# The first attention's maxima step in another ring of banks, and its transposed scores in front of the scores

## The chip, the cores and the metric

The kernel runs on one core of one Trainium2 chip. The time is device microseconds of that core. A run is one execution of the whole program; the times given are of three runs, and one further execution was taken with the hardware profiler.

## The reference

The program is a small stack of layers over x of shape 2 x 512 x 512 in float32: four attentions, each followed by a feed-forward layer, every layer on a layer norm of x and added to x. The change touches only the first attention, which has 32 heads of 4 latent columns and no mask:

```python
C_q = x @ Wq_d + bq_d                                   # 12 columns
C_kv = x @ Wkv_d + bkv_d                                # 4 columns
q = (C_q @ W_qk + b_qk).reshape(b, s, 32, 4)
scores = jnp.einsum('bqhd,bkd->bhqk', q, C_kv) / 2
attn = jax.nn.softmax(scores, axis=-1)
V = (C_kv @ Wv_u + bv_u).reshape(b, s, 32, 16)
out = jnp.einsum('bhqk,bkhd->bqhd', attn, V).reshape(b, s, 512)
return out @ Wo + bo
```

## The kernel before

Scores are computed twice. A score matmul has queries in its rows and keys in its columns (128 x 512); VectorE takes each row's negated maximum from it, and nothing else is kept. A transposed score has keys in its rows and queries in its columns; it goes through exp on ScalarE and is then the moving operand of the matmuls with the values. For the exp to see the maximum already taken off, the maxima themselves are transposed and added to the queries, as further rows of the moving operand qm.

The heads are handled four at a time, a *quartet*: 16 quartets, u = 0 to 15 (two batches, two halves, four each). The four heads g = 0 to 3 of a quartet lie on 32 partitions each, and a matmul of a score or of a transposed score reads only the 32 rows of its head.

- `score(u, qt, g)` (L586): a matmul of 32 rows (L589) into a bank of the S ring, then on VectorE a reduce of that bank into one column of `nm[u % 2]` (L597).
- `split(u)` (L601): two small GpSimd steps on the maxima (L606, L607), after the quartet's last score.
- `maxima(u)` (L611): four transposes of `nm` into one bank (L615), one more matmul that adds the queries (L199, in `correct`), and a copy on ScalarE to `qm[u]` (L618).
- `transposed(u, kc, g)` (L621): a matmul of 32 rows (L627) of `qm[u]` into a bank of the T ring, then exp on ScalarE (L630).
- `values(u, kc)` (L632): four matmuls of the values with the exps (L637), into a bank of their own.

The eight PSUM banks are dealt out by hand: the S ring has banks 0, 1, 2, the T ring 3, 4, 5, the values bank 6, and bank 7 takes other work. `own_bank` goes around a ring; a matmul into a bank waits until the reduce, exp or copy that read the bank's last content is done.

TensorE's instructions are issued in the order in which they are written here (`manual_schedule`); the other engines' order is the scheduler's. Twelve half rows of scores (`next_scores`, two matmuls each) are issued ahead; then every quartet has eight steps. A step has two scores of a later quartet, two transposed scores of this one, and then either a `values` of four heads or a slice of other work (`slices`: heads of the second batch, sums of weights, the feed-forward layer's first products, layer norms; two or three matmuls that fill up, if there is nothing). In even steps the scores are of heads 0 and 1 and the transposed scores of heads 2 and 3, in odd steps the other way around. Scores run 12 half rows ahead, so the maxima of quartet u + 1 are complete after step 3 of quartet u; `maxima(u + 1)` stands in step 6, and `transposed(u + 1, ...)` begins in step 0 of the next quartet. "Step 0" below is always that of the quartet that follows.

Of the kernel before, what the change touches and what calls it, by code (L numbers as in the profile page):

```python
# [38 lines left out]
B, S, D = 2, 512, 512  # L39
# [389 lines left out]
def attn_latent_small(k, a):  # L429
# [9 lines left out]
    with ExitStack() as ctx:  # L439
# [134 lines left out]
        last = len(quartets) - 1  # L574
# [7 lines left out]
        def own_bank(kind):  # L582
            turns[kind] = (turns[kind] + 1) % 3
            return k.held[:, banks[kind][turns[kind]]]

        def score(u, qt, g):  # L586
            b, half, i = quartets[u]
            ps = own_bank("S")
            nc.tensor.matmul(  # L589
                ps,  # L590
                qs[b][rows[g], 4 * half + i, bass.ts(qt, P)],
                keys[b][rows[g]],
                start=True,
                stop=True,
            )
            at = 32 * g + HIGH
            k.latest = nc.vector.tensor_reduce(  # L597
                nm[u % 2][:, qt, at : at + 1], ps, AX.X, ALU.max, negate=True
            ).ins

        def split(u):  # L601


            every = nm[u % 2].rearrange("p t (g e) -> p t g e", g=4)
            top = lp.tile([P, NT, 4], F32R, tag="top", name="top")
            nc.gpsimd.tensor_copy(top, every[:, :, :, HIGH])  # L606
            k.pooled = nc.gpsimd.tensor_tensor(  # L607
                every[:, :, :, LOW], every[:, :, :, HIGH], top.bitcast(F32), ALU.subtract
            ).ins

        def maxima(u):  # L611
            b, half, i = quartets[u]
            tp = own_bank("S")
            for qt in range(NT):
                nc.tensor.transpose(tp[:, bass.ts(qt, P)], nm[u % 2][:, qt], k.ident)  # L615
            k.correct(tp, unit, qs[b][:, 4 * half + i])
            t = lp.tile([P, S], F32R, tag="qm", name="qm")
            nc.scalar.copy(t, tp)  # L618
            qm[u] = t

        def transposed(u, kc, g):  # L621
            b, half, i = quartets[u]
            if (u, kc) not in probs:
                odd = kc % 2
                probs[u, kc] = lp.tile([P, 4, S], F32, tag="pT", name="pt") if odd else k.other()
            ps = own_bank("T")
            nc.tensor.matmul(  # L627
                ps, keys[b][rows[g], bass.ts(kc, P)], qm[u][rows[g]], start=True, stop=True
            )
            nc.scalar.activation(probs[u, kc][:, g], ps, AF.Exp)  # L630

        def values(u, kc):  # L632
            b, half, i = quartets[u]
            acc = k.held[:, of_values]
            pt = probs.pop((u, kc))
            for g in range(4):
                nc.tensor.matmul(  # L637
                    acc[rows[g]],
                    vals[b][:, kc, i],
                    pt[:, g],  # L640
                    start=(i == 0 and kc == 0),
                    stop=(i == 3 and kc == NT - 1),
                )
            if i == 3 and kc == NT - 1:
                raws[u] = one([P, S], "raw")
                nc.scalar.copy(raws[u], acc)
                extra.extend(following(u))
# [91 lines left out]
        def next_scores():  # L739
            at = next(scores, None)  # L740
            if at:
                u, qt, p = at
                for g in (2 * p, 2 * p + 1):
                    score(u, qt, g)
                if (qt, p) == (NT - 1, 1):
                    split(u)

        def run(pieces):
            for piece in pieces:
                for _ in piece:  # L750
                    pass

        def fill(n, bank):
            for _ in range(n):
                nc.tensor.matmul(k.held[:, bank], unit, keys[0], start=True, stop=True)

        def slices(cost):

            if not extra:
                fill(3, k.ring[-1])  # L760
            with tc.issue_after(first):
                while extra and cost > 0:
                    done = next(extra[0], None)
                    if done is None:
                        extra.pop(0)
                    else:
                        cost -= done
# [35 lines left out]
        with tc.manual_schedule(engines={mybir.EngineType.PE}):  # L803
            for n in range(12):
                next_scores()
                slices(1)
                fill(2, of_values)
                if n == 7:
                    with tc.issue_after(k.latest):
                        adapter_coefficients(k, a)  # L810
                if n == 8:
                    maxima(0)
            run(extra)
            extra = later
            k.ring = other
            for u in range(len(quartets)):
                if u == last:
                    k.ring = (0, 1, 2, 7)
                for step in range(8):
                    next_scores()  # L820
                    for g in (2, 3) if step % 2 == 0 else (0, 1):
                        transposed(u, step // 2, g)
                    if step == 6 and u < last:
                        maxima(u + 1)
                    if step % 2 == 0 and len(behind) > 1:
                        values(*behind.pop(0))
                        if u == last:
                            slices(1)
                    else:
                        slices(2 if u == last else 1)  # L830
                    if step % 2:
                        behind.append((u, step // 2))
            k.ring = (0, 1, 2, 3, 4, 5, 7)
            for at in behind:
                values(*at)
            run(extra)
# [4 lines left out]
def adapter_coefficients(k, a):  # L841

    nc = k.nc
    k.coef = k.const.tile([P, 1], F32, tag="coef", name="coef")
    starts = k.load_row(a["f0_starts"], 4, "f0_starts", dtype=I32)
    rows = k.load(a["c_lora"], [P, 4], "c_lora", 1)
    startf = k.sm(4, "startf", 1)
    nc.vector.tensor_copy(startf, starts)


    c = k.sm(4, "le", 1)
    nc.vector.tensor_scalar(c, startf, rows[:, 3:4], None, ALU.is_le)
    r = k.sm(3, "rank", 1)
    both = k.sm(2, "adapter", 1)
    nc.vector.tensor_tensor(both, c[:, 1:3], c[:, 2:4], ALU.mult)
    nc.vector.tensor_tensor(r[:, 0:2], c[:, 1:3], both, ALU.subtract)
    nc.vector.tensor_copy(r[:, 2:3], both[:, 1:2])
    nc.vector.tensor_tensor(r, r, rows[:, 0:3], ALU.mult)
    nc.vector.tensor_reduce(k.coef, r, AX.X, ALU.add)
# [1308 lines left out]
@with_exitstack  # L2168
def kernel(ctx: ExitStack, tc: tile.TileContext, a: dict, out: bass.AP):
    k = Block(ctx, tc, a["x"], out)  # L2170
    k.hold()
    block = attn_latent_small(k, a)
    bound = CausalBound(k, a)
    attn_gqa(k, a, bound, block)
    ffn_lora(k, a, block)
    attn_mla(k, a)
    k.release(ctx)
    with k.tc.tile_pool(name="f1", bufs=2) as own:
        experts = Experts(k, a, own)
        with k.tc.tile_pool(name="heads", bufs=1) as pool:  # L2180
            rooms = HeadRooms(k, a, pool)
            experts.first(rooms.fill)
            attn_mha(k, a, bound.register(), rooms, experts)
        experts.end()
# [168 lines left out]
```

## Time and profile before

| | us |
|---|---|
| median of 3 runs | 1969.8 |
| lowest and highest | 1969.27, 1971.89 |
| the profiled execution | 1968.03 |
| its span, first to last instruction | 1966.3 |
| TensorE busy in the span | 1926.5 |
| VectorE busy | 1372.1 |
| ScalarE busy | 933.6 |
| GpSimd busy | 1026.6 |
| mean granted TensorE clock | 0.999 |

In the profile PE is TensorE's matmuls, PEld its weight loads, DVE VectorE, ACT ScalarE, POOL GpSimd; L589 is line 589 of the kernel. A timeline row has the start in us, the time from start to end in us, engine, line, operation, what is written and read, shapes, and how many were merged; a bracket at the end tells how long the engine had been idle and what ended that. Matmuls overlap: the time from one matmul's start to the next one's, here called a slot, tells what it occupies TensorE for. A waits row has who waited, for whom, us in total, how often, and the longest. A windows row has, for each engine, its busy time and number of instructions in that stretch, then the granted clock and the DMA's share and rate.

The first attention's quartets run from about 42 to 255 us of the span.

### The profile page before, as it was taken

The numbers are of one execution on the slowest core, as the hardware profiler recorded it, in microseconds if no ns is written. First come the engines' busy times: TensorE is split into PE (matmuls) and PEld (weight loads), VectorE is DVE, ScalarE is ACT, GpSimd is POOL, SyncE is SP. The second block draws the span as 40 slices with busy tenths as digits, with TensorE's granted clock in tenths as the row PEclk, the third lists the DMA queues.
The fourth block names the chain that finished last, engine by engine and source line by source line (L and its number), as shares of the span: only waits on it lengthen the run. The fifth ranks groups of instructions, "written<-read, shape, count | busy, mean of one in ns | idle before, by whom it ended". The sixth has DMA issues, their size and how long they took to land.

```text
span 1966.3 us, 40477 instructions
## 1 busy us (share of the span) xinstructions
PE 1926.5 (98%) x15610; PEld 1194.0 (61%) x15610; DVE 1372.1 (70%) x3457; ACT 933.6 (47%) x2450; POOL 1026.6 (52%) x1122
## 2 busy tenths in 40 slices
PE   9989999999999999999999999999999999999999
PEld 5333356777777777777777545666565654654554
DVE  8889658767776676777765577777777756847853
ACT  3876624444444343444443166666666411541550
POOL 4332055776756667677763257565656556216221
PEclk9999999999999999999999999999999999999999
DMA  3010212222322322232223212020101002002001
GB/s 136 17 44 1 75 65 66 82 72 88 97 68 61 97 76 82 76 98 76 79 79 85 72 22 109 7 71 10 62 13 55 23 12 48 2 2 44 2 2 44
DMA packets 69296, 108.96 MB, mean 55 GB/s; under 512 B 13922, under 2 KB 48994, under 8 KB 62052
## 3 DMA queue, kind: packets, MB, share of 16 engines
q1 hardware_dynamic: 68804, 104.15, 18.0%
q8 instruction: 127, 2.08, 0.4%
q0 software_dynamic: 288, 2.10, 0.3%
q14 instruction: 77, 0.63, 0.1%
HBM read 80.00 MB, written 4.19 MB: 43 GB/s over the span
## 4 chain that ended last, share of the span: by engine, by line
PE 84%; DVE 6%; POOL 5%; issue 3%; ACT 2%; SPq 0%; DMA 0%; DVEq 0%; POOLq 0%; ACTq 0%
PE held L1004 13%; PE held L281 11%; PE held L1139 9%; PE held L190 9%; PE held L357 8%; PE held L637 3%; PE held L589 3%; PE held L1076 3%; PE held L473 2%; PE held L1498 2%; PE sc L190 2%; PE held L1495 1%; PE tp L1769 1%; DVE nm L597 1%; PE held L1496 1%
## 5 line engine op out<-in xcount | busy, mean ns | idle before, releaser
L302 ACT ACTIVATE room<-room,nmax 128x128 f32<-128x128 f32 (+3 forms) x384 | 212.7, 557 | 355.2 <-DVE nmax L292 352.7
L281 PE MATMUL held<-kT,q 128*32 128x32 f32 (+15 forms) x4096 | 262.6, 396 | 6.6 <-DVE invs L310 2.3
L292 DVE CUSTOM_DVE_ANT_0 room<-held,mask 128x128 f32<-128x128 f32 (+3 forms) x384 | 178.9, 488 | 63.1 <-PE held L281 57.7
L281 PEld LDWEIGHTS held<-kT,q 128*32 128x32 f32 x4096 | 143.1, 110 | 87.5 <-issue 34.7
L357 PE MATMUL held<-turned,vals 32*128 32x384 f32 (+7 forms) x2784 | 189.5, 416 | 1.5 <-issue 1.5
L597 DVE TENSOR_REDUCE nm<-held 128x1 f32<-128x512 f32 x256 | 161.7, 683 | 24.6 <-PE held L627 14.6
L357 PEld LDWEIGHTS held<-turned,vals 32*128 32x128 f32 (+1 forms) x2784 | 149.3, 167 | 40.2 <-issue 23.3
L315 ACT ACTIVATE room<-room,invs 128x128 f32<-128x128 f32 (+3 forms) x312 | 151.3, 551 | 41.0 <-DVE invs L310 40.9
L254 DVE TENSOR_TENSOR rows<-rows,held 128x512 f32<-128x512 f32 x198 | 129.5, 673 | 31.9 <-PE held L1004 31.3
L330 DVE STREAM_TRANSPOSE turned<-room 128x1152 f32<-128x1152 f32 x80 | 107.9, 1361 | 40.7 <-ACT room L315 21.6
L243 POOL TENSOR_TENSOR rstd<-ve,mhalf 128x1 f32<-128x1 f32 x64 | 36.3, 571 | 177.4 <-DVE ve L241 177.4
L1165 POOL TENSOR_TENSOR q<-q,room 128x256 f32<-128x256 f32 x64 | 45.3, 730 | 123.5 <-DVE q L1148 112.8
L1183 POOL TENSOR_TENSOR q<-q,cosq 128x512 f32<-128x512 f32 x60 | 88.1, 1468 | 31.5 <-DVE t L1180 31.5
L1139 PE MATMUL held<-room,w 128*128 128x256 f32 x384 | 95.0, 383 | 0.0
L1184 POOL TENSOR_TENSOR q<-q,t 128x512 f32<-128x512 f32 x64 | 86.8, 1356 | 6.3 <-DVE q L1183 2.5
L302 ACT ACTIVATE probs<-probs,nmax 128x128 f32<-128x128 f32 (+3 forms) x128 | 70.7, 553 | 40.2 <-DVE nmax L292 39.4
L589 PEld LDWEIGHTS held<-keys,qs 32*128 32x128 f32 x256 | 30.8, 182 | 95.1 <-DVE nm L597 66.6
L1004 PE MATMUL held<-w,ctxT 128*128 128x256 f32 x360 | 86.5, 383 | 0.1
L630 ACT ACTIVATE pt<-held 128x512 f32<-128x512 f32 x128 | 69.7, 598 | 30.9 <-PE held L627 25.7
L589 PE MATMUL held<-keys,qs 32*128 32x512 f32 x256 | 77.1, 497 | 5.5 <-DVE nm L597 5.1
L630 ACT ACTIVATE room<-held 128x512 f32<-128x512 f32 x128 | 69.7, 598 | 26.8 <-PE held L627 22.0
L1519 POOL TENSOR_TENSOR q<-t,t 64x512 f32<-64x512 f32 x62 | 78.9, 1273 | 4.9
(439 smaller groups left out, 4950.9 us busy)
## 6 DMA issues: line engine op xcount, KB each, us to landing
w<-in_b_wq SPq DMA_DIRECT2D x16, 1024.0 KB, 4.9
w<-in_b_wo SPq DMA_DIRECT2D x16, 1024.0 KB, 5.4
vals<-v SPq DMA_DIRECT2D x256, 64.0 KB, 2.1
w<-in_m_wo SPq DMA_DIRECT2D x8, 1024.0 KB, 6.9
w<-in_b_wk SPq DMA_DIRECT2D x16, 256.0 KB, 2.7
w<-in_b_wupv SPq DMA_DIRECT2D x16, 256.0 KB, 2.6
w<-in_m_wqn SPq DMA_DIRECT2D x8, 384.0 KB, 3.1
rows<-in_x SPq DMA_DIRECT2D x8, 256.0 KB, 4.1
```

The costliest lines, as they stand in the source:

```text
L190: last = self.nc.tensor.matmul(out, lhsT, rhs, start=(i == 0), stop=(i == len(pairs) - 1))
L254: self.nc.vector.tensor_tensor(x, x, ps.rearrange("p (t d) -> p t d", t=2), op)
L281: nc.tensor.matmul(ps[32 * i : 32 * i + 32, a - lo : b - lo], q[:, at : at + 32], keys[:, a:b], start=True, stop=True,)
L292: nc.vector.tensor_tensor_reduce(out=row, in0=ps[:, :kv], in1=self.mask_back[:, :kv] if qt % 2 else self.mask[:, S - kv :], op0=ALU.add, o ...
L302: nc.scalar.activation(row, row, AF.Exp, bias=nmax, scale=-1.0, accum_out=total[:, qt : qt + 1])
L315: self.nc.scalar.activation(row, row, AF.Identity, scale=each)
L357: self.nc.tensor.matmul(out[:, :, :n], values(i, j), rhs, start=(j == blocks[0]), stop=(j == stop[i]),)
L589: nc.tensor.matmul(ps, qs[b][rows[g], 4 * half + i, bass.ts(qt, P)], keys[b][rows[g]], start=True, stop=True,)
L597: k.latest = nc.vector.tensor_reduce(nm[u % 2][:, qt, at : at + 1], ps, AX.X, ALU.max, negate=True).ins
L630: nc.scalar.activation(probs[u, kc][:, g], ps, AF.Exp)
L1004: k.nc.tensor.matmul(out, lhsT[:, i, bass.ts(t, P)], rhs[i], start=not (after or t or i), stop=i == 1, skip_group_check=True,)
L1139: nc.tensor.matmul(out, lhsT[:, c], rhs[:, c], start=c == 0, stop=c == 1)
```

## The change

The maxima step takes its bank from the T ring instead of the S ring, and moves from step 6 to step 7. In steps 1 to 6 the two transposed scores are issued ahead of the two scores; in steps 0 and 7 the scores stay in front. In step 7 the maxima step stands between the scores and the transposed scores. The first quartet's maxima, issued in the lead, take a T bank too.

```diff
         def maxima(u):
             b, half, i = quartets[u]
-            tp = own_bank("S")
+            tp = own_bank("T")
             for qt in range(NT):
                 nc.tensor.transpose(tp[:, bass.ts(qt, P)], nm[u % 2][:, qt], k.ident)
             k.correct(tp, unit, qs[b][:, 4 * half + i])
...
                 for step in range(8):
-                    next_scores()
+                    ahead = step in (0, 7)
+                    if ahead:
+                        next_scores()
+                    if step == 7 and u < last:
+                        maxima(u + 1)
                     for g in (2, 3) if step % 2 == 0 else (0, 1):
                         transposed(u, step // 2, g)
-                    if step == 6 and u < last:
-                        maxima(u + 1)
+                    if not ahead:
+                        next_scores()
                     if step % 2 == 0 and len(behind) > 1:
                         values(*behind.pop(0))
                         if u == last:
```

## The prediction

> **What bounds the kernel now.** First the page: is one engine full, and does it also end the span?
>
> ```profile
> span 1966.3 us, 40477 instructions
> ...
> PE 1926.5 (98%) x15610; PEld 1194.0 (61%) x15610; DVE 1372.1 (70%) x3457; ACT 933.6 (47%) x2450; POOL 1026.6 (52%) x1122
> ...
> PE 84%; DVE 6%; POOL 5%; issue 3%; ACT 2%; SPq 0%; DMA 0%; DVEq 0%; POOLq 0%; ACTq 0%
> ```
>
> TensorE is 98% busy and carries 84% of the chain that ended last. The change touches only the first attention, so next the stage's windows; 42.1 and 255.1 are the first and the last start of the transposed scores (L627), to 1 us.
>
> ```profile
> core 0: us, PE busy (x) PEld busy (x) DVE busy (x) ACT busy (x) POOL busy (x), PEclk, DMA share, GB/s
> 42.10:255.10 213.00, 205.55 (x1220) 72.22 (x1220) 171.16 (x296) 154.10 (x290) 49.98 (x76) 0.99 0.10 36
> ```
>
> TensorE idles for 7.5 of 213 us, VectorE for 42, ScalarE for 59. Which idle could the change remove? TensorE's waits in that window:
>
> ```profile
> PE held L589 <- DVE nm L597: 4.7, 11, 0.6
> PE held L615 <- DVE nm L597: 1.3, 7, 0.2
> PE held L473 <- DVE wv_diag L542: 0.9, 1, 0.9
> PE held L655 <- ACT raw L646: 0.3, 1, 0.3
> ```
>
> The second line is the wait that another bank would end: 7 of 15 maxima transposes wait for a reduce to empty their S bank, 1.3 us in all. Read by starts in the timeline the seven are 0.26 us each, 1.8 us (a 0.43 us slot is over, then nothing starts for 0.26). Now TensorE's timeline around a maxima step without a wait:
>
> ```profile
> 221.37 0.50 PE L589 MATMUL held<-keys,qs 32*128 32x512 f32 x2
> 221.37 0.50 PE L627 MATMUL held<-qm,keys 32*128 32x512 f32 x2
> 221.84 0.63 PE L615 MATMUL held<-ident,nm 128*128 128x128 f32 x4
> 222.22 0.47 PE L199 MATMUL held<-qs,unit 128*128 128x512 f32 x1
> 222.63 1.06 PE L637 MATMUL held<-pt,vals 128*32 128x512 f32 x8
> 223.62 0.50 PE L589 MATMUL held<-keys,qs 32*128 32x512 f32 x2
> 224.06 1.12 PE L473 MATMUL held<-adapted,room 128*128 128x512 f32 x2
> 225.12 0.50 PE L589 MATMUL held<-keys,qs 32*128 32x512 f32 x2
> ```
>
> Two scores (L589) and two transposed scores (L627) start within 10 ns: each uses 32 of the array's 128 rows, and the four share one slot of 0.43 us (223.62 to 224.06). Call it a quad. A pair alone, where no scores are left, is no cheaper:
>
> ```profile
> 231.40 0.50 PE L627 MATMUL held<-qm,keys 32*128 32x512 f32 x2
> 231.83 0.64 PE L637 MATMUL held<-room,vals 128*32 128x512 f32 x4
> ```
>
> Slot 0.43 again. Last, a boundary between quartets where TensorE does wait:
>
> ```profile
> 125.68 0.50 PE L589 MATMUL held<-keys,qs 32*128 32x512 f32 x1 [0.42 <-DVE nm L597]
> 126.37 0.63 PE L615 MATMUL held<-ident,nm 128*128 128x128 f32 x4 [0.18 <-DVE nm L597]
> 127.16 1.06 PE L637 MATMUL held<-pt,vals 128*32 128x512 f32 x8
> 128.15 0.50 PE L589 MATMUL held<-keys,qs 32*128 32x512 f32 x2
> 129.43 0.50 PE L589 MATMUL held<-keys,qs 32*128 32x512 f32 x1 [0.56 <-DVE nm L597]
> 129.86 1.07 PE L637 MATMUL held<-room,vals 128*32 128x512 f32 x8
> ```
>
> The wait before 126.37 is the bank's; the one before 129.43 is step 0's second score, which needs the reduce of the score started at 128.15: 1.28 us from matmul to matmul over VectorE.
>
> **The change, part by part.** Steps 1 to 6: transposed scores go first. The quad stays a quad, so no slot is added. What moves is who holds up whom: scores now queue behind a wait for ScalarE. An exp starts 0.60 us after its matmul (93.35 to 93.94) and takes 0.60, so with 0.04 to the next start that wait ends 1.24 us after the matmul of the bank's earlier turn, against 1.28 for the reduce. The reduce still ends last; the first score of a split quad comes up to 0.8 us later, but VectorE then still works on the two before it (four reduces take 2.48 in a 2.70 us pair of steps, 0.22 idle). I take 0; if that cover fails, 0.2 for each of some 24 split quads, 4.8 us. A gain is excluded: only the exps come earlier, and nobody waits for those (the values that read them stand two steps later).
>
> Step 7 is where the price is. The quad is torn: scores, then the maxima step (four transposes, L199), then the transposed scores. The maxima cost 0.79 (221.84 to 222.63) before as after. Added is one slot of 0.43. Also added is one change between small row tiles and the full array: two L473 between quads take 1.06 (224.06 to 225.12), while twenty L190 in one row of the chain take 8.58, 0.43 each; 1.06 less 0.86 is 0.20 for the two changes, 0.10 each. So 0.52 where TensorE never waits.
>
> The Trainium skill, "TensorEngine Tiling (Array Packing)", Key Properties, states that a change of tiling mode drains TensorE, and so speaks against this change. It gives no figure; with no drain at all the price would be 0.43.
>
> The added wait: step 0's second transposed score takes the bank of step 7's first one. Counted from the first maxima transpose at m: that matmul starts at m+0.89 (0.79 and a change of mode), its exp at 1.49 (ScalarE has begun the copy qm at about 0.95, and a next one follows after 0.49), and the bank is free 1.24 after the matmul, at m+2.13. The first needs qm itself, by m+1.60. Queued behind on TensorE are only step 0's values; its scores stand in front. Between lie the pair (0.43), a slice of other work and the scores, so a slice of 0.87 or more hides it.
>
> Boundary by boundary (start of maxima in the timeline of before; 15, one a quartet):
> - 51.82, 181.26, 195.01, 221.84: no wait, slices of 1.06 or 1.71: 0.52 each, 2.08.
> - 88.85 and 114.50: no wait at the maxima, small slices (0.43 and none). Maxima would start at 90.24 and 115.90, the bank be free at 92.37 and 118.03, against second scores at 91.91 and 117.57 before: 0.46 each, 0.92.
> - 64.49, 126.37, 138.24, 209.54: both waits. At 126.37: before, from the quad at 125.68 to step 0's last pair 3.75. After: 0.43, values 1.00, scores 0.43, then 2.13: 3.99. 0.24 each, 0.96.
> - 76.35 and 150.95: 0.52 less the bank wait 0.26; at 76.35 the scores must wait 0.10 more for reduces: 0.62 together.
> - 100.97: L473 waits till 104.20 for L542, which hangs on POOL: the new slot fits inside. 0.
> - 165.32: VectorE has no gap from 157.3 to 180.9; TensorE's slot goes into waits. Between 0 and 0.3; 0.05, by the gapless rows.
> - 234.74: no scores are left, only the change of mode, 0.10.
>
> Sum 4.73 us. Moved too are reduces and one copy, on engines with 42 and 59 us idle; no DMA; the small POOL steps stay three steps ahead of the maxima. In the lead the first maxima leave the S ring: 0 to 0.2 gain, taken as 0. After 255 nothing is tied to absolute time (DMA 20% busy), so the delay reaches the end. The profiled execution took 1968.0 (span 1966.3 and 1.7 around it): 1972.7. The median of the runs lies 1.8 higher, 1969.8: **1974.5**.
>
> One loose term: granted clock. In 150 to 153 us it is 0.81, in 153 to 156 0.62; the values at 151.74 take 1.80 instead of 1.00, the next quad 0.73, four transposes 1.04 for 0.59: 1.6 us lost. The change moves the idle ahead of it, so it may go or come twice: 1.6 either way.
>
> The Trainium skill, "TensorE: Matmul & The Clock Gate", Part 1, says that the gate judges activity in free-running windows of about 3.4 us. By it the phase is chance, and the term noise from run to run.
>
> **Rivals.** About 0.2% (3.9 us) is what a measurement of this kernel can tell from no change.
> - *More is hidden* (no measurable change): VectorE's backlog swallows the slot also at 181.26, 195.01 and 221.84, whose neighbourhoods hold gapless stretches (185.9 to 194). 4.73 less 1.56 is 3.2; with the clock's better side 1.6. Near 1972. Against it: VectorE idles 0.4 to 1.3 in exactly these boundaries.
> - *VectorE sets the pace* (faster): now it starves at a boundary (1.27 idle before the reduce at 128.69, against the usual 0.22) since maxima and values separate the scores; with scores ahead of the maxima 1.05 could come back at the four double-wait boundaries and two single ones, 6.3 us: 1963.5. It decides only if step 0's pair needn't wait for m+2.13, and TensorE's own slots leave room; rows with 7.5 us TensorE idle against 42 speak against it.
> - *Scores starve behind ScalarE* (slower still): the 4.8 of steps 1 to 6 comes on top: 1979.4. For it: exps delayed by other copies (a 0.27 hold at 97.58). Against: 1.24 is under 1.28.
>
> **How the numbers follow.** Forecast 0.56, more hidden 0.29, VectorE 0.08, starving 0.07. Slower by over 0.2%: 0.56 and 0.07, 0.63; within: 0.29; faster: 0.08. The forecast's own range: all six no-wait boundaries at 0.43 and the double-wait ones at 0.2 give 4.1; all 14 boundaries with scores at 0.52 give 7.3: 1973.9 to 1977.1. The whole range runs from 1970.3 (more hidden, the clock's good side, and runs 1.3 apart) to 1978.5, leaving out VectorE and about half of starving.
>
> **What would show it.** In the changed profile: the L615 wait on nm gone; at each boundary L589 x2 alone, L615, L199, L627 x2 alone, 0.43 and 0.43; a wait of step 0's L627 for ScalarE about 2.13 after the first L615 where slices are small; the stage longer by 4 to 6 us and the rest equal. Wrong if a torn pair costs under 0.3 where TensorE doesn't wait, if L627's waits for ScalarE appear in steps 1 to 6, or if the stage after 255 gives time back.

## The result, and the profile after

The changed kernel is slower: median 1979.0 us of 6 runs (1974.62 to 1980.36) against 1969.53 of 6 runs before. The ratio is 1.0042, 95% interval 1.0032 to 1.0052, or some 8.3 us; the medians lie 9.5 us apart. A second set of 5 runs gave 1978.1 against 1969.4, ratio 1.0043 (1.0030 to 1.0056). The way was forecast, the size was not: 1974.5 was forecast, with a range up to 1978.5; the first set's median lies 0.5 us above its end, the second's 0.4 us below.

The profiled execution took 1974.62, the shortest of the six; its span is 6.6 us longer than before's. The page's head, TensorE's row and the chain:

```profile
span 1972.9 us, 40460 instructions
...
PE 1935.0 (98%) x15610; PEld 1200.0 (61%) x15610; DVE 1372.2 (70%) x3457; ACT 932.2 (47%) x2450; POOL 1024.9 (52%) x1122
...
PE 83%; POOL 6%; DVE 5%; issue 3%; ACT 2%; DMA 0%; SPq 0%; DVEq 0%; POOLq 0%; ACTq 0%
```

The same 15610 matmuls take 8.5 us more of TensorE. The windows row of the first attention, which now lasts from 42.1 to 260.7 (first to last transposed score, to about 1 us, as before), and TensorE's waits in it:

```profile
42.10:260.70 218.60, 212.39 (x1219) 77.08 (x1223) 171.48 (x296) 153.29 (x290) 49.59 (x76) 1.00 0.10 35
```

```profile
PE held L627 <- ACT room L630: 2.6, 6, 0.4
PE held L589 <- DVE nm L597: 1.4, 2, 1.1
PE held L627 <- ACT pt L630: 0.9, 2, 0.4
PE held L473 <- DVE wv_diag L542: 0.7, 1, 0.7
PE held L627 <- ACT wv_diag L513: 0.3, 1, 0.3
PE held L655 <- ACT raw L646: 0.3, 1, 0.3
```

The stage is 5.6 us longer (218.6 against 213.0), although before's holds a stretch at half clock and this one none. Its idle has shrunk a little (6.2 against 7.5): TensorE is not kept waiting longer, it is busy for 6.8 us more. The maxima's wait for a reduce (L615) is gone. The transposed scores (L627) wait for ScalarE where the scores (L589) waited for VectorE. One wait of 1.1 us for VectorE is new. A boundary of the sort shown before, without waits:

```profile
227.01 1.06 PE L637 MATMUL held<-pt,vals 128*32 128x512 f32 x8
228.00 0.50 PE L589 MATMUL held<-keys,qs 32*128 32x512 f32 x2
228.43 0.65 PE L615 MATMUL held<-ident,nm 128*128 128x128 f32 x4
228.84 0.47 PE L199 MATMUL held<-qs,unit 128*128 128x512 f32 x1
229.24 0.49 PE L627 MATMUL held<-qm,keys 32*128 32x512 f32 x2
229.67 1.13 PE L473 MATMUL held<-adapted,room 128*128 128x512 f32 x2
230.72 0.50 PE L589 MATMUL held<-keys,qs 32*128 32x512 f32 x2
```

There is the torn quad: the scores alone from 228.00 to 228.43, the maxima to 229.24, the transposed scores alone to 229.67. Each pair has a slot of 0.43.

**A measure for all kernels.** A profile holds half-clock windows of 3.41 us, some of them two on end, in places that differ from one execution to the next (before's has one at 151.9, the changed kernel's one at 1168.8). A window costs at most half its length, 1.7 us. So I take from each timeline the start of the first values matmul of quartet 0 and that of quartet 15, subtract half of the length of half-clock windows between them, and compare with before. This *growth* of the quartets is 6.63 us in the profile of the changed kernel, and 6.68 in a second one. Kernels with the same order agree within 0.1.

For before's own window half the length is too much. Here are the values behind the maxima at 150.95 and the next quartet's first values, in before's profile and then in that of e8 (below), which has the same order there and no window:

```profile
151.74 1.87 PE L637 MATMUL held<-pt,vals 128*32 128x512 f32 x8
162.04 0.64 PE L637 MATMUL held<-room,vals 128*32 128x512 f32 x4
```

```profile
151.04 1.06 PE L637 MATMUL held<-pt,vals 128*32 128x512 f32 x8
160.03 0.64 PE L637 MATMUL held<-room,vals 128*32 128x512 f32 x4
```

That is 10.30 us against 8.99, so the window cost 1.31 and not 1.71: the slow stretch swallowed, for one, a wait of 0.26 for VectorE. Every growth in the table, and above all the part of it at 150.95, is therefore some 0.4 us too high. Differences between two kernels are not touched. The growths of e2 and e7 are the least sure, since their profiles hold windows of their own among the quartets.

| kernel | growth, us | median, us | ratio (95% interval) |
|---|---|---|---|
| changed | 6.63 | 1979.0 | 1.0042 (1.0032 to 1.0052) |
| changed, again (e5) | 6.68 | 1978.1 | 1.0043 (1.0030 to 1.0056) |
| bank alone (e1) | -0.42 | 1970.0 | 1.0001 (0.9992 to 1.0010) |
| order of pairs alone (e2) | 2.87 | 1973.2 | 1.0016 (1.0007 to 1.0025) |
| tear alone (e3) | 4.43 | 1973.6 | 1.0022 (1.0012 to 1.0031) |
| changed, quad whole (e4) | 1.34 | 1970.6 | 1.0009 (1.0000 to 1.0018) |
| changed, copy held back (e6) | 5.68 | 1975.9 | 1.0047 (1.0024 to 1.0070) |
| step 3 torn (e7) | 12.53 | 1988.4 | 1.0102 (1.0089 to 1.0116) |
| bank alone, lead in S (e8) | -0.48 | 1968.2 | 0.9993 (0.9985 to 1.0002) |
| changed, lead in S (e9) | 6.60 | 1975.9 | 1.0033 (1.0021 to 1.0046) |
| maxima behind the quad (e10) | -0.18 | 1969.4 | 0.9994 (0.9985 to 1.0003) |
| maxima between (e11) | 4.38 | 1973.1 | 1.0019 (1.0010 to 1.0028) |
| e8 again (e12) | -0.51 | 1968.6 | 0.9995 (0.9986 to 1.0004) |

### The profile page after: what moved, and what is told of

Same layout as the page of the kernel before. It is cut to its first block, busy times and chain, and to the rows that moved or that the text cites. A ratio compares the mean times of both kernels' runs of the same rounds, so it can differ in the third digit from the quotient of the medians.

```text
span 1972.9 us, 40460 instructions
## 1 busy us (share of the span) xinstructions
PE 1935.0 (98%) x15610; PEld 1200.0 (61%) x15610; DVE 1372.2 (70%) x3457; ACT 932.2 (47%) x2450; POOL 1024.9 (52%) x1122
## 4 chain that ended last, share of the span: by engine, by line
PE 83%; POOL 6%; DVE 5%; issue 3%; ACT 2%; DMA 0%; SPq 0%; DVEq 0%; POOLq 0%; ACTq 0%
PE held L1008 13%; PE held L281 11%; PE held L1143 9%; PE held L190 8%; PE held L357 8%; PE held L637 3%; PE held L1080 3%; PE held L627 2%; PE held L473 2%; PE held L1502 2%; PE sc L190 2%; PE held L1499 1%; PE tp L1773 1%; PE held L1500 1%; PE sc L2093 1%
## 5 line engine op out<-in xcount | busy, mean ns | idle before, releaser
L2107 POOL TENSOR_SCALAR_AFFINE_SELECT room<-room 128x512 f32<-128x512 f32 x32 | 20.3, 635 | 117.0 <-ACT room L2103 111.5
L1143 PEld LDWEIGHTS held<-room,w 128*128 128x128 f32 x384 | 71.5, 190 | 14.3 <-issue 2.0
L1520 POOL TENSOR_TENSOR t<-t,sinq 128x512 f32<-128x512 f32 x31 | 39.8, 1284 | 76.7 <-DVE invs L310 65.9
```

The lines of the kernel that those rows point to most:

```text
L1143: nc.tensor.matmul(out, lhsT[:, c], rhs[:, c], start=c == 0, stop=c == 1)
```

## The experiments

The expectations name theory A, the torn quad and a copy in VectorE's order; theory B, that scores starve behind transposed scores; and theory C, that half-clock windows have become more frequent.

**e1: the bank alone.**

```diff
-            tp = own_bank("S")
+            tp = own_bank("T")
```

> Only the bank: maxima stay in step 6 behind the quad, but in a T bank. Theory A (the torn quad of step 7 costs 0.52 us a boundary, and in the changed kernel a bias copy, L560, that VectorE's order puts in front of the reduces costs 1.4 us once): the seven waits of L615 for a reduce go, 1.8 us less; 0.3 us more at the first transposed scores, whose bank the lead's heads still hold; median about 1968. Theory B (transposed scores in front of scores starve VectorE): the same, since the order of scores is untouched. If the bank itself is harmful, over 1971.

Growth -0.42 (-0.8 with before's window at its cost), and no difference in time, where 1968 was expected. The waits of L615 vanished from the list, but of their 1.8 us the quartets kept less than half: five of the seven boundaries gain 0.07 to 0.16 each instead of 0.26. Starts in the timeline tell why. Before, the maxima began 0.68 us after the last quad at all seven boundaries; in e1 they begin 0.42 after it at 150.95, but still 0.54 to 0.58 at the other six, each time 0.14 us after the end of the exp that last read their T bank. Half of the wait stayed, for ScalarE instead of VectorE, as gaps of 0.1 us or less that the list leaves out. TensorE's waits for reduces (L589) stay at 4.7 us, 11 times, as before.

**e2: the order of the pairs alone.**

```diff
-                    next_scores()
+                    ahead = step in (0, 7)
+                    if ahead:
+                        next_scores()
                     for g in (2, 3) if step % 2 == 0 else (0, 1):
                         transposed(u, step // 2, g)
+                    if not ahead:
+                        next_scores()
                     if step == 6 and u < last:
                         maxima(u + 1)
```

> Only the order: in steps 1 to 6 the transposed scores stand in front of the scores; maxima stay in step 6, behind both, in an S bank. Theory A: the quad is a quad either way; VectorE's order has the bias copy L560 in front of the reduces as in the changed kernel, so one wait of L589 over 1 us near 77 us; 1.4 us more than before, about 1971, and L627's waits for ScalarE in steps 1 to 6 under 1 us in all beyond that. Theory B: 4 us or more over before, 1974 and up, spread over the split quads of 62 to 150 us.

Growth 2.87, between the two. One step, quartet 2 to 3, holds 1.33 of it (the copy, see e6); the other 1.5 comes in pieces of 0.06 to 0.55 in quartets that have split quads (0.4 of the 0.55 is before's window). Neither theory had a price for that; it stands below, under the second point.

**e3: the tear alone.**

```diff
                     next_scores()
+                    if step == 7 and u < last:
+                        maxima(u + 1)
                     for g in (2, 3) if step % 2 == 0 else (0, 1):
                         transposed(u, step // 2, g)
-                    if step == 6 and u < last:
-                        maxima(u + 1)
```

and the T bank as in e1.

> Only the tear: scores in front in every step, maxima in a T bank and in step 7 between the scores and the transposed scores. VectorE's order keeps L560 behind the reduces. Theory A: 4.7 us for the tear and 0.3 at the start, about 1974.5, no wait of L589 near 1 us. Theory B: at most 1 us over before, below 1971.

Growth 4.43 and 1973.6, as theory A had it; theory B falls as the main cause.

**e4: the changed kernel with a whole quad.**

```diff
-                    if ahead:
-                        next_scores()
                     if step == 7 and u < last:
                         maxima(u + 1)
+                    if ahead:
+                        next_scores()
```

> The changed kernel with step 7's quad whole again: maxima first, then scores and transposed scores together. Theory A: against the changed kernel 4.7 to 6 us less; against before 1.8 less for the bank waits, 1.4 more for L560, 0.3 more at the start: 1969.5 within 1. Theory B: still 1974 or more. Theory C (what lifts the changed kernel's runs from 1974.6 to 1980.3 is more windows of half clock, about 1.7 us each, since TensorE idles more between 120 and 160 us): granted clock 0.999 here, and runs within 2 us of each other.

Growth 1.34, of which 1.24 in the one step with the copy; against the changed kernel 5.3 less. The median is 1970.6, where 1969.5 within 1 was expected. Of theory C: the mean granted clock over the runs is 0.9982, like before's, but single runs spread over 5 us.

**e6: the copy.** In the changed kernel VectorE has an idle time that before's lacks:

```profile
73.74 2.51 DVE L597 TENSOR_REDUCE nm<-held 128x1 f32<-128x512 f32 x4 [0.29 <-PE held L589]
77.58 0.43 DVE L560 COPY wv_diag<-a_bvu 128x512 f32<-128x512 f32 x1 [1.34 <-POOL qs L482]
77.94 1.27 DVE L597 TENSOR_REDUCE nm<-held 128x1 f32<-128x512 f32 x2
```

The scheduler, which orders VectorE, has put the bias copy of `fold_bias` four reduces earlier than before: behind 66 reduces instead of 70. Every kernel with the new order of pairs, but e6, has it behind 66; the others have it behind 70 or 72. The copy's buffer is still read by GpSimd (L482), so it waits, and the reduces behind it wait too: that is the 1.1 us of L589 in the waits. e6 holds the copy back:

```diff
-            nc.vector.tensor_copy(bv_rep, bvu.unsqueeze(2).broadcast_to([P, KC, P]))
+            with tc.issue_after(k.latest):
+                nc.vector.tensor_copy(bv_rep, bvu.unsqueeze(2).broadcast_to([P, KC, P]))
```

> The changed kernel with the bias copy L560 ordered behind the latest reduce on VectorE; TensorE's order is the same. Theory A: the one wait of L589 over 1 us goes, 1.4 us less than the changed kernel beside it, last values 5.9 us later than before's. If the copy had been harmless, no difference.

In its profile VectorE works through the same place (lines are one higher in this kernel):

```profile
74.14 2.48 DVE L598 TENSOR_REDUCE nm<-held 128x1 f32<-128x512 f32 x4 [0.60 <-PE held L590]
76.91 2.51 DVE L598 TENSOR_REDUCE nm<-held 128x1 f32<-128x512 f32 x4 [0.29 <-PE held L590]
```

The last values stand 6.1 us after before's (5.9 was expected), and the growth falls by 0.96 to 5.68, where 1.4 was expected: held back, the copy is itself waited for once, 0.4 us, by a slice of other work (L473). The times can't show it: the ratio's interval is 46 hundredths of a per cent wide, because two of the ten runs took 1992.6 us at a granted clock of 0.987.

**e7: another quad torn.** Before, with step 3's slice of other work between its scores and its transposed scores, and the copy held back as in e6:

```diff
                     next_scores()
+                    if step == 3:
+                        slices(2 if u == last else 1)
                     for g in (2, 3) if step % 2 == 0 else (0, 1):
...
-                    else:
+                    elif step != 3:
                         slices(2 if u == last else 1)
```

> The kernel before with the quad of step 3 torn by that step's slice of other work: scores, slice, transposed scores; L560 held behind the reduces; maxima, banks and order of all else as before. Theory A: 0.43 us in the seven or eight quartets whose slice is two full matmuls and where TensorE doesn't wait, 0 where the slice has no matmul or the next score waits for a reduce anyway: 3.0 to 3.9 us over before, about 1973.2. Theory B: no cost, below 1970.5, since the order of scores is untouched.

Growth 12.53, three to four times what was expected, and theory B is no nearer. The timeline shows what was left out (score L590, transposed score L628):

```profile
60.42 0.49 PE L590 MATMUL held<-keys,qs 32*128 32x512 f32 x2
60.84 1.12 PE L473 MATMUL held<-room,w 128*128 128x512 f32 x2
61.90 0.50 PE L628 MATMUL held<-qm,keys 32*128 32x512 f32 x3
62.23 0.39 PE L590 MATMUL held<-keys,qs 32*128 32x512 f32 x2
63.07 0.49 PE L628 MATMUL held<-qm,keys 32*128 32x512 f32 x1 [0.45 <-ACT pt L631]
63.50 0.64 PE L638 MATMUL held<-room,vals 128*32 128x512 f32 x4
```

The torn pair of step 3 now stands next to step 4's, four transposed scores in a ring of three banks. The fourth, at 63.07, waits for the exp of the first, at 61.90: 1.17 us, the chain over ScalarE. From 60.42 to the values it takes 3.08; two quads of 0.43 and the slice of 1.06 are 1.92. So here the tear costs its slot, and the ring's turn on top, since it brings two pairs of one kind together; the other quartets were not taken apart like this.

**e8 and e12: the bank alone, the lead's maxima in an S bank** (the same kernel in two sets).

```diff
-            tp = own_bank("S")
+            tp = own_bank("T" if u else "S")
```

> Only the bank, and the first quartet's maxima, those issued in the lead, stay in an S bank. Theory A: the first transposed scores no longer wait for a head's copy out of their bank, 0.3 to 0.6 us less than the bank alone; last values 0 to 0.5 us earlier than before's, time the same as before within noise.

> Once more, beside the others: before with the maxima of all but the first quartet in a T bank. Theory A: last values 0.4 us earlier than before's, time 0.7 to 1.3 us less, at the edge of what the runs can tell.

Growth -0.48 and -0.51; ratios 0.9993 and 0.9995, both intervals holding 1. This is the version that the experiments point to. By the traces it is 0.5 us better than before, or 0.9 with before's window at its cost; the runs can't tell it from before.

**e9: the changed kernel with the lead in S; e5: the changed kernel once more.**

> The changed kernel, with the lead's maxima back in an S bank. Theory A: 0.5 us less than the changed kernel, by last values 6.7 us after before's. Theory C in a narrower form (the lead's wait near 42 us starves TensorE just enough for half-clock windows at 43 us, which stand in four of the five profiles with the lead's maxima in a T bank and in none without): no window there, mean granted clock back at before's 0.998, median near 1976.

> The changed kernel once more, beside its variants. With half-clock windows counted off (half of each window's length), its last values stand 7.3 us later than before's. Theory A: 7 to 8 us over before in the medians, so about 1977, with single runs 1.7 us apart by windows. Theory C (the tear makes windows of half clock more frequent): 9 us or more over before, most runs at a granted clock of 0.996 or 0.997.

Growth 6.60 and 6.68; the lead's bank changes nothing in the quartets. e5's median is 8.6 us over before's, between what theories A and C had. e9 had no window at 43 us, but its mean clock was 0.9977 over 6 runs, and its median 1975.9.

**e10 and e11: the tear by itself.** Scores in front in every step, the same banks, the maxima (in T banks, the lead's in S) in step 7 behind the quad (e10) or inside it (e11); this is the edit from e10 to e11:

```diff
                     next_scores()
-                    for g in (2, 3) if step % 2 == 0 else (0, 1):
-                        transposed(u, step // 2, g)
                     if step == 7 and u < last:
                         maxima(u + 1)
+                    for g in (2, 3) if step % 2 == 0 else (0, 1):
+                        transposed(u, step // 2, g)
```

> Scores in front everywhere, whole quads, maxima in a T bank behind step 7's quad (the lead's in S). Theory A: no torn quad, so as fast as before or a little faster: the maxima fill the wait that step 0's second score has in six boundaries; last values 0.4 to 1.5 us earlier than before's, 1968 to 1969.5. If what costs is the maxima's place in step 7, so near the first use of qm, and not the tear: 4 us over before.

> The same kernel as the one with the maxima behind step 7's quad, but with the maxima between its scores and its transposed scores: the tear alone, same step, same banks, same order of VectorE. Theory A: 4 to 5 us slower than that one, last values 4 us after before's. If the tear is harmless: the same time.

The two timelines at the same boundary, e10 first:

```profile
221.15 0.50 PE L589 MATMUL held<-keys,qs 32*128 32x512 f32 x2
221.16 0.50 PE L627 MATMUL held<-qm,keys 32*128 32x512 f32 x2
221.59 0.66 PE L615 MATMUL held<-ident,nm 128*128 128x128 f32 x4
222.00 0.48 PE L199 MATMUL held<-qs,unit 128*128 128x512 f32 x1
222.32 1.02 PE L473 MATMUL held<-adapted,room 128*128 128x512 f32 x2
223.27 0.50 PE L589 MATMUL held<-keys,qs 32*128 32x512 f32 x2
```

```profile
225.66 0.50 PE L589 MATMUL held<-keys,qs 32*128 32x512 f32 x2
226.09 0.66 PE L615 MATMUL held<-ident,nm 128*128 128x128 f32 x4
226.50 0.47 PE L199 MATMUL held<-qs,unit 128*128 128x512 f32 x1
226.91 0.50 PE L627 MATMUL held<-qm,keys 32*128 32x512 f32 x2
227.34 1.12 PE L473 MATMUL held<-adapted,room 128*128 128x512 f32 x2
228.39 0.49 PE L589 MATMUL held<-keys,qs 32*128 32x512 f32 x2
```

From scores to scores 2.12 and 2.73 us: 0.43 for the pair's own slot, 0.18 where in e10 the maxima and the slice, both on the full array, follow each other without a pair between them (maxima 0.73 instead of 0.82, slice 0.95 instead of 1.05). e10's last values stand 0.3 us before before's (0.7 with before's window at its cost; 0.4 to 1.5 was expected). Growth 4.56 apart, medians 3.8. The maxima's place in step 7 is harmless; standing inside the quad is what costs.

## Why the prediction was right and wrong

**The torn quad, right.** Forecast 4.73; the kernels with the tear and without the new order of pairs grew by 4.43 (e3) and 4.38 (e11), or 4.0 with before's window at its cost. In the changed profile the torn pair's second half starts 0.81 to 0.82 us after the first transpose at all 15 boundaries (0.89 was forecast), and where slices are small step 0's second transposed score starts 2.06 after it, seven times (2.13 was forecast). By quartets, in the changed kernel, e11 and the forecast: 51.82, 0.49, 0.41 and 0.52; 88.85, 0.65, 0.55 and 0.46; 100.97, 0.05, -0.02 and 0; 126.37, 0.32, 0.15 and 0.24; 165.32, 0.00, -0.02 and 0.05; 195.01, 0.53, 0.49 and 0.52; 234.74, 0.00, 0.02 and 0.10. So the slot that waits hide and the slot that they don't were told apart by the rows of before. 150.95 seems not to fit (0.70 in e11 against 0.26), but 0.40 of it is before's window. Two don't fit: 138.24 (-0.25 against 0.24), which stays open, and 76.35 (0.75 against 0.36), where e11's waits have the copy again:

```profile
PE held L473 <- DVE wv_diag L560: 0.4, 1, 0.4
```

**The added change of mode, mis-sized.** The sum had 0.10 for it. In the changed profile scores, maxima and transposed scores take 0.43, 0.81 and 0.43 (228.00 to 229.67), against quad and maxima 1.26 before (221.37 to 222.63): 0.41 more, no drain added. The four boundaries without waits measured 0.36 to 0.49 in e11. The 0.10 came from L473, another matmul, between quads. The Trainium skill, "TensorEngine Tiling (Array Packing)", Key Properties, says that changing the mode drains TensorE. e10 agrees, where one visit to the full array less saves 0.18; the maxima's own new change shows nothing. The page has no number, so rows alone decide which change costs.

**Steps 1 to 6 at 0, wrong.** e6 less e3 is 1.25, and e2 without the copy's step 1.5, or 1.1 without before's window. One of the prediction's own signs of being wrong came: L627 waits for ScalarE eight times in steps 2, 4 and 6, 0.38 to 0.44 us each. The step that failed is the comparison of 1.24 us for the exp "against 1.28 for the reduce", out of which it took 0. The reduce does still end last; but the comparison tied the two latencies to the engines. Here are the exp (ACT) and the reduce (DVE) that answer the quad at 124.39 before, scores first:

```profile
125.00 0.60 ACT L630 ACTIVATE room<-held 128x512 f32<-128x512 f32 x1 [0.38 <-PE held L627]
124.93 2.48 DVE L597 TENSOR_REDUCE nm<-held 128x1 f32<-128x512 f32 x4 [0.23 <-PE held L627]
```

and those of the quad at 126.15 in the changed kernel, transposed scores first, with TensorE's rows:

```profile
126.15 0.49 PE L627 MATMUL held<-qm,keys 32*128 32x512 f32 x2
126.16 0.50 PE L589 MATMUL held<-keys,qs 32*128 32x512 f32 x2
126.68 0.60 ACT L630 ACTIVATE pt<-held 128x512 f32<-128x512 f32 x1 [0.70 <-PE held L589]
126.75 2.51 DVE L597 TENSOR_REDUCE nm<-held 128x1 f32<-128x512 f32 x4 [0.28 <-PE held L589]
127.33 0.50 PE L627 MATMUL held<-qm,keys 32*128 32x512 f32 x1 [0.44 <-ACT pt L630]
127.33 0.65 PE L589 MATMUL held<-keys,qs 32*128 32x512 f32 x2
127.91 1.06 PE L637 MATMUL held<-room,vals 128*32 128x512 f32 x8
128.91 0.49 PE L627 MATMUL held<-qm,keys 32*128 32x512 f32 x2
```

Whoever reads the pair that is issued first starts 0.53 to 0.54 us after it (124.39 to 124.93; 126.15 to 126.68), whoever reads the second 0.59 to 0.61 (124.40 to 125.00; 126.16 to 126.75). With the order turned, the longer chain, over VectorE, also gets the later start. The wait for the exp ends at 127.33, after 1.18 us; of the two scores in the row at 127.33 the second starts 0.16 later, 1.33 us after the score at 126.16, where this took 1.28 before. So a pair of steps takes 2.76 (126.15 to 128.91) instead of 2.70. Some 13 pairs of steps in quartets 2 to 8 are 0.05 to 0.09 longer in e6 than in e3, 0.9 us together; the rest of the 1.25 is what remains of larger gains and losses, mostly in quartets 0, 1 and 8 to 11, and was not traced. The rival "starving" had the right place, but 4.8 as its price and another mechanism: in these rows the wait for ScalarE ends before the reduce's.

**What the forecast did not have.** The bias copy's new place costs 0.96 to 1.0 (changed against e6). The edit touched only TensorE's hand-written order, and the forecast took the other engines' order as given ("reduces and one copy", at nothing); with the new order of pairs the scheduler chose another for VectorE. Do the parts add up? e3 has the tear without the new order, e2 the new order, with its copy, without the tear: 4.43 and 2.87 are 7.30, against 6.63 for both at once. Quartet by quartet the two sum to the changed kernel's within 0.1, but for 76.35 (2.11 against 1.79; e3 too has a wait of 0.4 for the copy) and 150.95 (1.26 against 0.86; before's window is in it twice).

**The clock, open.** Growth explains 6.2 (with before's window at its cost) to 6.6 of 8.3 to 9.5 us. If from each run's time the part lost to the granted clock is taken (time by one less the mean clock, told to 0.001), the medians are 1966.1 before and 1972.4 after, 6.3 apart; the rest is the clock. Its mean is 0.9982 over 81 runs of before, 0.9971 over 11 of the changed kernel and 0.9977 over 6 of e9, but 0.9985 and 0.9987 in e3 and e11. e6 has 0.9961, but by two of its ten runs alone (0.987); the other eight have 0.9984, with the tear and the new order in them. The windows are not in one place, though some places come back: of the 14 profiles nine have one between 1809 and 1829 us and four one between 1161 and 1169. Two of the four stretches in e5's profile:

```profile
43.20:50.10 6.90, 6.90 (x15) 2.10 (x15) 2.98 (x6) 2.94 (x6) 1.84 (x2) 0.51 0.00 0
1760.00:1763.60 3.60, 3.60 (x25) 1.22 (x28) 0.00 (x0) 1.02 (x6) 1.27 (x2) 0.53 0.00 0
```

The first lies just behind the lead. A window at 43 to 44 us stands in five of the six profiles with the lead's maxima in a T bank (all but the changed kernel's first) and in none of the eight with them in an S bank; in all six a first transposed score waits 0.3 us for ScalarE at 43 us (L513). So the lead's bank seems to bring that one window, but with e9, which has none there in its profile, the clock's deficit didn't go. That windows may move was forecast (1.6 either way, from rows at half clock; before's cost 1.31); why the changed kernel has more of them is not shown.

**The rivals.** "More is hidden" fell at 195.01, where the tear was paid in full. "VectorE sets the pace" fell: three of the four double-wait boundaries lost 0.28 to 0.38 in the changed kernel; only 138.24 gained, 0.14.

## What to carry to other kernels

Where small matmuls share the array only because they stand next to each other, price anything that is put between them at a whole slot, and look up in the trace whether a pair alone costs as much as the group. A wait that vanishes from the waits view need not be gone: here half of it stayed at most boundaries, for another engine and too short for the view to list, so look at when the instruction starts, and who last read its new bank. And after a change to one engine's order, compare the order of the engines that nobody wrote by hand.

## What was not expected of the hardware

Of two pairs of matmuls issued within 10 ns, the reader of the second starts 0.06 us later, whichever engine it is. The medians, over readers that had been idle: an exp 0.59 us after the second pair (64 in before's profile) and 0.53 after the first (41 in the changed kernel's), a reduce 0.59 after the second (25 in the changed kernel's) and 0.53 after the first (36 in before's). Granted clock falls to half in stretches of 3.41 us even while TensorE is busy 98% of the span, at places that change from run to run, though some come back. The Trainium skill, "TensorE: Matmul & The Clock Gate", Part 1, has free-running windows of about 3.4 us; the length agrees (3.41).
